# A gated cross-attention block: one slot's scores and the rounding of w1 are moved in the start-up, and the rounding takes two operations

## The chip, the core and the metric

The kernel runs on one core of a Trainium2 chip. The core has five engines with an in-order queue of instructions each: TensorE (PE, matrix products and transposes), VectorE (DVE), ScalarE (ACT), GpSimd (POOL) and SyncE (SP, which here only starts transfers). They meet by semaphores. The metric is the time of one execution on the device in microseconds (us).

## The reference

A Flamingo block: 16 batches of 224 tokens of width 512 attend to 750 context rows of width 384 each, of which a mask keeps a part (8 heads of 64); then comes a feed-forward net whose two weights are rounded to -1, 0 and 1 and whose activations are rounded to 8 bits.

```python
def weight_quant(w):
    scale = 1.0 / jnp.clip(jnp.mean(jnp.abs(w)), 1e-05)
    return jnp.clip(jnp.round(w * scale), -1.0, 1.0) / scale
def bitlinear(x, w, b):                       # act_quant: 127 steps to each row's largest
    return jnp.einsum('bsd,fd->bsf', act_quant(rmsnorm(x)), weight_quant(w)) + b
x = x + tanh(g_xattn) * xattn(layernorm(x), ctx, mask, W_q, W_k, W_v, W_o, b_o)
y = layernorm(x)                              # w1: 2048 x 512, w2: 512 x 2048
x = x + tanh(g_ffn) * bitlinear(gelu(bitlinear(y, w1, b1)), w2, b2)
```

## The kernel before, in words

**Slots.** A first stage (`order_batches`, with an SBUF pool `sel` of its own) sorts the 16 batches by how many context rows they keep, into 16 slots: eight of up to 192 kept rows, eight of up to 128. From then on only kept rows are loaded: `select` (indicators L816, key numbers L833, mask L845; its small products L822 on PE) works out a slot's rows, `gather` (L856) fetches them with indirect DMAs that POOL issues, and `fetch` does so for tokens (L793).

**A slot.** Tokens are handled in pairs of 128-row tiles that run across slots. `norm` layer-normalises a pair (statistics on the DVE, L952 and L953; the rest on POOL: L956, L959, a power L780 and the normalisation L961); `norm_first` does slot 0's on its own. `turn` (L987) transposes a tile on PE, `query_pieces` makes the queries (L1008), `context_pieces` transposes context rows (L881) and makes keys (L892) and values (L907, and L918 for rows above 128). `scores(s, n)` takes unit n of four, 112 tokens by four heads: products `sim` on PE (L1047), scaled, masked and with its maximum taken in one DVE instruction per head (L1061), the exponential with its sum on ACT (L1071), the sums' reciprocals on the DVE (L1080), and the product of both on POOL (L1081), all in a buffer `p`. `turn_probs` transposes a `p` on PE (L1101, L1108), `weighted` multiplies by the values. Pairs of 128 rows then go through projection (L1189), a second norm, `up` (L1259), the gelu, and `down` (L1304).

**Weights.** w1 and w2 come in eight chunks of 128 x 1024 float32 each. A chunk of w2 takes over the buffer `raw` of a w1 chunk once that is rounded. `sum_weights` adds up absolute values (even chunks on the DVE, L1363, odd ones on ACT, L1367, whose elementwise output goes to a scratch tile `junk`); `scale_weights` adds the sums over partitions with a product on PE (`wtotp`, L1375) and makes the scale `sw`. `round_weights` (L1396 to L1398) rounds a chunk into `w16`, of which there are three; `turn_weights` transposes it on PE (L1409 for w1, L1413 for w2) into the 8-bit weights `w1T`, `w2T` (copies L766 on ACT or L763 on the DVE: `evict` takes the one with the smaller running sum, `load["s"]` and `load["v"]`).

**The order.** The start is written out: fetch, select and gather of slot 0, its norm, loads of w1, queries, keys and values; slot 0's scores 0 and 1; the sums of w1 and its scale; then slot 1's norm pieces and `select(2)`; then the remaining loads (wo, bo, b1, b2). After that a loop runs over slots. In a slot s, `merge` interleaves three lists of pieces by their costs: `attention_pieces(s)` (with scores 2 and 3 of the slot between the turns), the preparation of the following slots, and, for s of 0 and 1, `weight_pieces(s)` (w1 with slot 0, w2 with slot 1), from slot 2 on the projection and the feed-forward net. At its end come scores 0 and 1 of slot s + 1. At s = 2 bo and b2 are multiplied by the gates on POOL (L1519, L1520).

This order of calls isn't yet the engines' order. The framework's scheduler places each engine's instructions in its queue by their readiness in its own model, so an instruction written later may come earlier, and `tc.issue_after(i)` holds those written under it behind instruction i. In the built kernel before, POOL's queue after p of units 0 and 1 holds: statistics and normalisation of x_1, two gathers of slot 2, the multiply of bo, that of b2, the normalisation of x_2, four indirect loads, then p of units 2 and 3.

Of the kernel before, what the change touches and what calls it, by code (L numbers as in the profile page):

```python
# [8 lines left out]
F32 = mybir.dt.float32  # L9
BF16 = mybir.dt.bfloat16  # L10
AF = mybir.ActivationFunctionType
ALU = mybir.AluOpType
# [17 lines left out]
def order_batches(ctx, tc, sh, mask, x, context):  # L30

    nc = tc.nc
# [3 lines left out]
    NJ = 6  # L36
    TJ = J // NJ
    const = sh.const
    sel = ctx.enter_context(tc.tile_pool(name="sel", bufs=1))
    ps = ctx.enter_context(tc.tile_pool(name="ps_sel", bufs=1, space=bass.MemoryType.PSUM))  # L40

    m8 = sel.tile([B, J], mask.dtype, name="m8")
# [683 lines left out]
def compact_path(ctx, tc, sh, x, context, out, late_loads):  # L726

    nc = tc.nc
    P = 128
    B, S, D = x.shape  # L730
    _, J, C = context.shape
    FF = sh.FF
    NQ = 2
    TQ = S // NQ
# [9 lines left out]
    I32 = mybir.dt.int32  # L744
    I16 = mybir.dt.int16
# [3 lines left out]
    pa = ctx.enter_context(tc.tile_pool(name="pa", bufs=1))  # L749
# [3 lines left out]
    load = {"v": 0.0, "s": 0.0}  # L753

    latest = {}
# [15 lines left out]
    def wide(shape, dtype, name):  # L771
        return ps_sim.tile(shape, dtype, tag="sim", name=name)
# [9 lines left out]
    def small(name, n=2):  # L782
        return pa.tile([P, n], F32, tag=f"s{n}", name=name, bufs=24 if n == 2 else 6)
# [181 lines left out]
    def norm_first(k):  # L965

        xp = normed[0]
        st = small(f"bs_x0_{k}", 6)
        nc.vector.bn_stats(st, xp[:, k, :])
        mv = small(f"mv_x0_{k}", 4)  # L970
        nc.vector.bn_aggr(mv[:, :2], st)
        rstd = small(f"rs_x0_{k}")
        nc.vector.tensor_scalar(rstd[:, :1], mv[:, 1:2], EPS, None, ALU.add)
        power = nc.gpsimd.tensor_tensor(rstd[:, :1], rstd[:, :1], sh.mhalf[:, :1], ALU.pow)
        nc.vector.tensor_scalar(xp[:, k, :], xp[:, k, :], mv[:, 0:1], rstd[:, :1], ALU.subtract, ALU.mult)
        return power.ins

    def slot_xnT(s):
        if "xnT" not in live[s]:
# [57 lines left out]
    def scores(s, n):  # L1037
        st = live[s]
        cap = CAPS[s]
        q, u = UNITS[n]  # L1040
        sim = wide([TQ, 2, 2, 256], F32, f"sim_{s}_{n}")

        begin = P if cap > P else 0
        for i in range(2):
            p = 2 * u + i
            for j in range(2):
                nc.tensor.matmul(  # L1047
                    sim[:, j, i, :cap],
                    lhsT=st["qT"][j * DH : (j + 1) * DH, p, q * TQ : (q + 1) * TQ],
                    rhs=st["kT"][j * DH : (j + 1) * DH, p, j * begin : j * begin + cap],  # L1050
                    start=True,
                    stop=True,
                )
        probs = pa.tile([TQ, 4, 192], F32, tag="p", name=f"p_{s}_{n}", bufs=3)
        total = small(f"sum_{s}_{n}", 4)
        for i in range(2):
            for j in range(2):
                h = 2 * i + j
                nmax = pa.tile([TQ, 1], F32, tag="nm", name=f"nm_{s}_{n}_{h}", bufs=12)

                nc.vector.tensor_tensor_reduce(  # L1061
                    out=probs[:, h, :cap],
                    in0=sim[:, j, i, :cap],
                    in1=st["mask"][:, j * begin : j * begin + cap],
                    scale=-(DH**-0.5),
                    scalar=FMAX,
                    op0=ALU.add,
                    op1=ALU.min,
                    accum_out=nmax,
                )  # L1070
                nc.scalar.activation(  # L1071
                    probs[:, h, :cap],
                    probs[:, h, :cap],
                    AF.Exp,
                    bias=nmax,
                    scale=-1.0,
                    accum_out=total[:TQ, h : h + 1],
                )
        rec = small(f"rec_{s}_{n}", 4)
        nc.vector.reciprocal(rec[:TQ], total[:TQ])  # L1080
        nc.gpsimd.tensor_tensor(  # L1081
            probs[:, :, :cap],
            probs[:, :, :cap],
            rec[:TQ].unsqueeze(2).to_broadcast([TQ, 4, cap]),
            ALU.mult,
        )
        load["v"] += 4 * (150 + 1.05 * cap + 83) + 150
        load["s"] += 4 * (250 + 0.96 * cap + 187)
        st["p", n] = probs

    def turn_probs(s, n):
        st = live[s]
        q, u = UNITS[n]
        cols = slice(q * TQ, (q + 1) * TQ)
        probs = st.pop(("p", n))
        if n == 0:
            st["pT"] = pa.tile([P, 12, S], F32, tag="pT", name=f"pT_{s}", bufs=1)
        pt = gen([P, 4, TQ], F32, f"ptp_{s}_{n}")
        for h in range(4):
            c = CAPS[s] - P if h % 2 else 0  # L1100
            nc.tensor.transpose(pt[:, h, :], probs[:, h, c : c + P], ident[:TQ, :TQ])  # L1101
        evict(st["pT"][:, 4 * u : 4 * u + 4, cols], pt, 4 * TQ)
        if CAPS[s] > P:

            pt = gen([P, 2, TQ], F32, f"ptr_{s}_{n}")
            for i in range(2):
                c = 2 * i * 192 + P
                nc.tensor.transpose(  # L1108
                    pt[:, i, :], probs.rearrange("t h k -> t (h k)")[:, c : c + P], ident[:TQ, :TQ]
                )  # L1110
            evict(st["pT"][:, 8 + 2 * u : 10 + 2 * u, cols], pt, 2 * TQ)
# [40 lines left out]
    def attention_pieces(s):  # L1152
        a = 4.0 if CAPS[s] > P else 2.6
        t = 0.8 if CAPS[s] > P else 0.5
        c = 1.4 if CAPS[s] > P else 1.0

        def both(n):
            scores(s, n)
            scores(s, n + 1)

        def wait():
            pass

        pieces = [(3.0, wait)]
        pieces += [(t, lambda n=n: turn_probs(s, n)) for n in (0, 1)]
        pieces += [(c, lambda: both(2)), (3.0, wait)]
        pieces += [(t, lambda n=n: turn_probs(s, n)) for n in (2, 3)]
        pieces += [(1.0, wait), (a, lambda: weighted(s))]
        return pieces
# [186 lines left out]
    def sum_weights(wi, c):  # L1356
        if c == 0:
            weight_sums.append(pa.tile([P, NPC], F32, name=f"wsums_{wi}"))
        if c == 1:
            late["junk"] = pa.tile([P, FF], F32, tag="h", name=f"junk_{wi}", bufs=2)  # L1360
        raw = raws[wi, c]
        if c % 2 == 0:
            nc.vector.tensor_reduce(  # L1363
                weight_sums[wi][:, c : c + 1], raw, AX.X, ALU.add, apply_absolute_value=True
            )
        else:
            nc.scalar.activation(late["junk"][:, :W], raw, AF.Abs, accum_out=weight_sums[wi][:, c : c + 1])  # L1367

    weight_scale = [None, None]
# [22 lines left out]
    def round_weights(wi, c):  # L1392

        raw = raws.pop((wi, c))
        quantised[wi, c] = w16 = pa.tile([P, W], BF16, tag="xq", name=f"w16_{wi}_{c}", bufs=3)
        nc.vector.tensor_scalar(raw, raw, weight_scale[wi], 1.0, ALU.mult, ALU.min)  # L1396
        nc.vector.tensor_scalar(w16.bitcast(I16), raw, -1.0, None, ALU.max)
        nc.vector.tensor_copy(w16, w16.bitcast(I16))  # L1398
        load["v"] += 1700

    def turn_weights(wi, c):
        w16 = quantised.pop((wi, c))
# [14 lines left out]
    def weight_pieces(wi):  # L1417

        p = []
        if wi == 1:  # L1420
            p += [(0.0, lambda: scale_weights(1))]
        for c in range(NPC + 2):
            if c < NPC:
                p += [(0.2, lambda c=c: round_weights(wi, c))]
                if wi == 0:
                    p += [(0.0, lambda c=c: load_weights(1, c))]
            if c > 1:
                p += [(0.6, lambda c=c: turn_weights(wi, c - 2))]
                if wi == 0:
                    p += [(0.0, lambda c=c: sum_weights(1, c - 2))]  # L1430
        return p
# [32 lines left out]
    select(0)  # L1464
    gather(0)
    select(1)
    norm_first(0)
    with tc.issue_after(norm_first(1)):
        fetch(1)
        gather(1)  # L1470
        fetch(2)
# [11 lines left out]
    with ExitStack() as behind:  # L1483
        for instruction in latest.values():
            behind.enter_context(tc.issue_after(instruction))
        scores(0, 0)
        scores(0, 1)
        for _, piece in queries[3:] + keys_values[3:]:
            piece()
        for c in range(NPC):  # L1490
            sum_weights(0, c)
        scale_weights(0)
        for _, piece in norm_pieces(1):
            piece()
        select(2)

        held = [sh.wo[0:1, 0, 0:1], sh.wo[0:1, 2, 0:1], sh.wo[P // 2 : P // 2 + 1, 2, 0:1]]
        for dst in held + [sh.bo[0:1, 0:1], sh.b1[0:1, 0:1], sh.b2[0:1, 0:1]]:
            nc.scalar.copy(dst, weight_sums[0][0:1, NPC - 1 : NPC])
# [85 lines left out]
```

## Time and profile before

| | |
|---|---|
| median of three runs | 756.2 us (754.46, 756.2, 758.74) |
| the profiled execution | 755.32 us |
| span of its trace | 753.5 us |
| mean granted PE clock | 0.976 of full speed |
| busy PE / DVE / ACT / POOL | 680.1 / 505.9 / 407.6 / 397.0 us |
| w1's last chunk landed, sums done | 36.0 us, 37.2 us |
| the queries (L1008) ahead of PE's longest wait | 54.28 to 57.38 us |
| PE's longest waits between 36 and 110 us | 5.1 for POOL's p, 3.6 for w2's first chunk, 1.7 for w1's first chunk |

Times are microseconds from the start of the span, unless marked ns. A line of a timeline gives start, length, engine, source line, operation, what is written and read with its shape, and how many instructions the line gathers. A line of waits gives who waits for whom: total, count and mean. A line of windows gives the stretch and its length, then the busy time of PE, of PE's weight loads, of DVE, ACT and POOL (instructions in brackets), the granted PE clock as a share of full speed, the share of the DMA engines and GB/s. The chain follows the work that ended last back from the end, each step to what released it; "issue" is time in which an engine waited for nothing that the profile shows. Numbers of buffers are left out of names (`x`, `raw`, `p`).

### The profile page before, as it was taken

The numbers are of one execution on the slowest core, as the hardware profiler recorded it, in microseconds if no ns is written. First come the engines' busy times: TensorE is split into PE (matmuls) and PEld (weight loads), VectorE is DVE, ScalarE is ACT, GpSimd is POOL, SyncE is SP. The second block draws the span as 40 slices with busy tenths as digits, with TensorE's granted clock in tenths as the row PEclk, the third lists the DMA queues.
The fourth block names the chain that finished last, engine by engine and source line by source line (L and its number), as shares of the span: only waits on it lengthen the run. The fifth ranks groups of instructions, "written<-read, shape, count | busy, mean of one in ns | idle before, by whom it ended". The sixth has DMA issues, their size and how long they took to land.

```text
span 753.5 us, 11378 instructions
## 1 busy us (share of the span) xinstructions
PE 680.1 (90%) x3902; PEld 432.9 (57%) x3902; DVE 505.9 (67%) x1300; ACT 407.6 (54%) x960; POOL 397.0 (53%) x543
## 2 busy tenths in 40 slices
PE   4997799999999999997999999999999999988652
PEld 3875587666566566555655575666666666443221
DVE  5598765877484784665768676588594939586860
ACT  1556564384663855736657369266565656460530
POOL 6583567464564644647266564565654453536141
PEclk9998999999999999999999999999999999999887
DMA  6874031132223322222142323123122222213150
GB/s 193 314 267 156 11 90 45 15 73 56 69 47 70 82 56 57 67 57 81 28 99 67 71 67 68 32 77 80 58 57 70 56 70 57 71 28 77 35 113 31
DMA packets 87218, 58.77 MB, mean 78 GB/s; under 512 B 75488, under 2 KB 75632, under 8 KB 87024
## 3 DMA queue, kind: packets, MB, share of 16 engines
q1 hardware_dynamic: 79024, 32.00, 18.8%
q0 software_dynamic: 8128, 25.96, 11.1%
q8 instruction: 33, 0.54, 0.3%
q14 instruction: 33, 0.27, 0.1%
HBM read 32.26 MB, written 7.34 MB: 53 GB/s over the span
## 4 chain that ended last, share of the span: by engine, by line
PE 57%; DVE 12%; issue 10%; POOL 9%; DMA 5%; ACT 2%; POOLq 0%; ACTq 0%; DVEq 0%; SPq 0%
PE qp L1008 9%; PE op L1189 9%; PE fp L1304 8%; PE hp L1259 6%; PE kp L892 5%; PE sim L1047 4%; PE vp L907 4%; PE ptp L1101 3%; PE av L1126 3%; DVE a L1282 2%; POOL p L1081 2%; DVE h L1267 2%; DMA raw<-in_L_ffn_w_dram 2%; DMA hqT<-hq 2%; DVE hq L1285 1%
## 5 line engine op out<-in xcount | busy, mean ns | idle before, releaser
L1081 POOL TENSOR_TENSOR p<-p,rec 112x768 f32<-112x768 f32 (+1 forms) x64 | 84.2, 1318 | 74.8 <-DVE rec L1080 29.6
L1304 PE MATMUL fp<-w2T,hqT 128*128 128x512 fp8e4 x448 | 104.2, 387 | 13.8 <-DMA hqT<-hq 13.7
L1259 PE MATMUL hp<-w1T,xqT 128*128 128x512 fp8e4 x448 | 107.0, 383 | 8.8 <-DVE h L1267 6.2
L1071 ACT ACTIVATE p<-p,nm 112x192 f32<-112x192 f32 (+1 forms) x256 | 106.4, 419 | 11.5 <-DVE nm L1061 11.3
L1008 PE MATMUL qp<-xnT,wq_sb 128*128 128x224 f32 x512 | 104.9, 358 | 0.6 <-ACT xnT L766 0.6
L1189 PE MATMUL op<-wo_sb,xoT 128*128 128x512 f32 x224 | 103.7, 599 | 0.0
L1008 PEld LDWEIGHTS qp<-xnT,wq_sb 128*128 128x128 f32 x512 | 96.8, 193 | 6.4 <-issue 3.3
L1267 DVE SCALAR_TENSOR_TENSOR h<-hp,c,b_bc 128x1024 f32<-128x1024 f32 x56 | 71.6, 1280 | 39.9 <-PE hp L1259 37.4
L1061 DVE CUSTOM_DVE_ANT_0 p<-sim,mask 112x192 f32<-112x192 f32 (+1 forms) x256 | 67.7, 319 | 33.9 <-PE sim L1047 33.4
L1304 PEld LDWEIGHTS <-hqT 128*128 128x128 bf16 x448 | 43.3, 99 | 71.0 <-DMA hqT<-hq 16.9
L1282 DVE TENSOR_REDUCE a<-h 128x1 f32<-128x2048 f32 x28 | 63.9, 2282 | 22.4 <-ACT h L1279 22.3
L1259 PEld LDWEIGHTS <-xqT 128*128 128x128 bf16 x448 | 43.2, 98 | 57.7 <-issue 15.4
L1308 DVE SCALAR_TENSOR_TENSOR y<-fp,c,y 128x512 f32<-128x512 f32 x28 | 20.9, 746 | 76.3 <-PE fp L1304 73.0
L1310 POOL DMA_INDIRECT out_dram<-y,token x28 | 30.9, 1104 | 75.6 <-DVE y L1308 70.6
L1290 ACT ACTIVATE h<-h 128x2048 f32<-128x2048 f32 x28 | 53.4, 1907 | 22.1 <-DVE hq L1285 14.7
L1279 ACT ACTIVATE h<-h 128x2048 f32<-128x2048 f32 x28 | 53.5, 1909 | 19.6 <-DVE k L1200 10.6
L1189 PEld LDWEIGHTS op<-wo_sb,xoT 128*128 128x128 f32 x224 | 40.6, 190 | 38.9 <-issue 36.4
L892 PE MATMUL kp<-ctxT,wk_sb 128*128 128x192 f32 (+1 forms) x384 | 60.9, 306 | 0.0
L892 PEld LDWEIGHTS kp<-ctxT,wk_sb 128*128 128x128 f32 x384 | 55.2, 192 | 6.2 <-issue 4.3
L1247 POOL TENSOR_TENSOR y<-y,b_bc 128x512 f32<-128x512 f32 x28 | 36.6, 1311 | 37.9 <-DVE fx L1228 37.6
L766 ACT COPY pT<-ptp 128x448 f32<-128x448 f32 x63 | 32.7, 536 | 42.6 <-PE ptp L1101 41.3
L1101 PE MATMUL ptp<-ident,p 112*128 112x112 f32 x256 | 36.1, 268 | 17.6 <-POOL p L1081 17.5
(165 smaller groups left out, 1191.4 us busy)
## 6 DMA issues: line engine op xcount, KB each, us to landing
raw<-in_L_ffn_w_dram SPq DMA_DIRECT2D x16, 512.0 KB, 5.6
wq_sb<-in_L_xattn_W_q_dram SPq DMA_DIRECT2D x1, 1024.0 KB, 5.8
b_bc<-in_L_ffn_b_dram SPq DMA_DIRECT2D x1, 1024.0 KB, 7.8
wk_sb<-in_L_xattn_W_k_dram SPq DMA_DIRECT2D x1, 768.0 KB, 7.4
wv_sb<-in_L_xattn_W_v_dram SPq DMA_DIRECT2D x1, 768.0 KB, 8.8
wo_sb<-in_L_xattn_W_o_dram SPq DMA_DIRECT2D x1, 512.0 KB, 3.8
wo_sb<-in_L_xattn_W_o_dram SPq DMA_DIRECT2D x2, 256.0 KB, 5.6
x<-in_x_dram,token POOLq DMA_INDIRECT x28, 3.6
```

What stands on the lines that cost most here:

```text
L892: nc.tensor.matmul(pk[:, p - p0, :], lhsT=sh.wk[:, c, p * P : (p + 1) * P], rhs=st["ctxT"][:, c, :cap], start=(c == 0), stop=(c == NC - 1),)
L1008: nc.tensor.matmul(pq[:, i, :], lhsT=sh.wq[:, d, (p + i) * P : (p + i + 1) * P], rhs=st["xnT"][:, d, :], start=(d == 0), stop=(d == ND - 1),)
L1061: nc.vector.tensor_tensor_reduce(out=probs[:, h, :cap], in0=sim[:, j, i, :cap], in1=st["mask"][:, j * begin : j * begin + cap], scale=-(DH ...
L1071: nc.scalar.activation(probs[:, h, :cap], probs[:, h, :cap], AF.Exp, bias=nmax, scale=-1.0, accum_out=total[:TQ, h : h + 1],)
L1081: nc.gpsimd.tensor_tensor(probs[:, :, :cap], probs[:, :, :cap], rec[:TQ].unsqueeze(2).to_broadcast([TQ, 4, cap]), ALU.mult,)
L1101: nc.tensor.transpose(pt[:, h, :], probs[:, h, c : c + P], ident[:TQ, :TQ])
L1189: nc.tensor.matmul(po, lhsT=xoT[:, d, at : at + P], rhs=sh.wo[:, d, :], start=(d == 0), stop=(d == ND - 1))
L1259: nc.tensor.matmul(ph[:, n, :], lhsT=f["xqT"][:, k * ND + d, :], rhs=w1T[:, d, at : at + NB], start=(d == 0), stop=(d == ND - 1),)
L1267: nc.vector.scalar_tensor_tensor(h[:, cols], ph.rearrange("t i n -> t (i n)"), f["c1", k], sh.b1[:, cols], ALU.mult, ALU.add)
L1279: nc.scalar.activation(f["h", k], f["h", k], AF.Gelu)
L1282: nc.vector.tensor_reduce(amax[:, k : k + 1], h, AX.X, ALU.max, apply_absolute_value=True)
L1304: nc.tensor.matmul(po, lhsT=f["hqT", k][:, n, :], rhs=w2T[:, n, :], start=(n == 0), stop=(n == NF - 1))
```

## The change

1. The pool `sel` of the sorting stage is taken from the other end of SBUF, so that its buffers lie apart from the first tokens' and context's.
2. `norm_first` also returns its last instruction: the second half of slot 0's tokens is normalised behind the first, and the fetches that follow are held behind the power in the second half.
3. `p` has four buffers in place of three.
4. Units 2 and 3 of slot 0's scores are called right behind its queries, keys and values, before the sums of w1; `attention_pieces(0)` has an empty piece in their place. The last DVE maximum of them is kept as `scored`.
5. Of w2's sums, chunks 0 and 4 are the DVE's and six are ACT's (before, four and four). w1's stay four and four.
6. Rounding: w times the scale into int32 (in the buffer `raw` itself), then the minimum with 1 and maximum with -1 into the bfloat16 `w16`. Before, there were three operations: scale and minimum in float32, maximum into int16, int16 to bfloat16. The planner's cost is 1400 instead of 1700.
7. The rounding of w1 is held behind `scored`.

```diff
--- before.py
+++ after.py
@@ -36,7 +36,8 @@
     NJ = 6
     TJ = J // NJ
     const = sh.const
-    sel = ctx.enter_context(tc.tile_pool(name="sel", bufs=1))
+
+    sel = ctx.enter_context(tc.tile_pool(name="sel", bufs=1, side="right"))
     ps = ctx.enter_context(tc.tile_pool(name="ps_sel", bufs=1, space=bass.MemoryType.PSUM))
 
     m8 = sel.tile([B, J], mask.dtype, name="m8")
@@ -972,8 +973,8 @@
         rstd = small(f"rs_x0_{k}")
         nc.vector.tensor_scalar(rstd[:, :1], mv[:, 1:2], EPS, None, ALU.add)
         power = nc.gpsimd.tensor_tensor(rstd[:, :1], rstd[:, :1], sh.mhalf[:, :1], ALU.pow)
-        nc.vector.tensor_scalar(xp[:, k, :], xp[:, k, :], mv[:, 0:1], rstd[:, :1], ALU.subtract, ALU.mult)
-        return power.ins
+        last = nc.vector.tensor_scalar(xp[:, k, :], xp[:, k, :], mv[:, 0:1], rstd[:, :1], ALU.subtract, ALU.mult)
+        return power.ins, last.ins
 
     def slot_xnT(s):
         if "xnT" not in live[s]:
@@ -1051,14 +1052,14 @@
                     start=True,
                     stop=True,
                 )
-        probs = pa.tile([TQ, 4, 192], F32, tag="p", name=f"p_{s}_{n}", bufs=3)
+        probs = pa.tile([TQ, 4, 192], F32, tag="p", name=f"p_{s}_{n}", bufs=4)
         total = small(f"sum_{s}_{n}", 4)
         for i in range(2):
             for j in range(2):
                 h = 2 * i + j
                 nmax = pa.tile([TQ, 1], F32, tag="nm", name=f"nm_{s}_{n}_{h}", bufs=12)
 
-                nc.vector.tensor_tensor_reduce(
+                latest["max"] = nc.vector.tensor_tensor_reduce(
                     out=probs[:, h, :cap],
                     in0=sim[:, j, i, :cap],
                     in1=st["mask"][:, j * begin : j * begin + cap],
@@ -1067,7 +1068,7 @@
                     op0=ALU.add,
                     op1=ALU.min,
                     accum_out=nmax,
-                )
+                ).ins
                 nc.scalar.activation(
                     probs[:, h, :cap],
                     probs[:, h, :cap],
@@ -1163,7 +1164,7 @@
 
         pieces = [(3.0, wait)]
         pieces += [(t, lambda n=n: turn_probs(s, n)) for n in (0, 1)]
-        pieces += [(c, lambda: both(2)), (3.0, wait)]
+        pieces += [(c, lambda: both(2) if s else wait()), (3.0, wait)]
         pieces += [(t, lambda n=n: turn_probs(s, n)) for n in (2, 3)]
         pieces += [(1.0, wait), (a, lambda: weighted(s))]
         return pieces
@@ -1359,7 +1360,7 @@
         if c == 1:
             late["junk"] = pa.tile([P, FF], F32, tag="h", name=f"junk_{wi}", bufs=2)
         raw = raws[wi, c]
-        if c % 2 == 0:
+        if c % (2 + 2 * wi) == 0:
             nc.vector.tensor_reduce(
                 weight_sums[wi][:, c : c + 1], raw, AX.X, ALU.add, apply_absolute_value=True
             )
@@ -1393,10 +1394,17 @@
 
         raw = raws.pop((wi, c))
         quantised[wi, c] = w16 = pa.tile([P, W], BF16, tag="xq", name=f"w16_{wi}_{c}", bufs=3)
-        nc.vector.tensor_scalar(raw, raw, weight_scale[wi], 1.0, ALU.mult, ALU.min)
-        nc.vector.tensor_scalar(w16.bitcast(I16), raw, -1.0, None, ALU.max)
-        nc.vector.tensor_copy(w16, w16.bitcast(I16))
-        load["v"] += 1700
+        nc.vector.tensor_scalar(raw.bitcast(I32), raw, weight_scale[wi], None, ALU.mult)
+        nc.vector.tensor_scalar(w16, raw.bitcast(I32), 1.0, -1.0, ALU.min, ALU.max)
+        load["v"] += 1400
+
+    def round_behind(wi, c):
+        if wi:
+            round_weights(wi, c)
+        else:
+
+            with tc.issue_after(scored):
+                round_weights(wi, c)
 
     def turn_weights(wi, c):
         w16 = quantised.pop((wi, c))
@@ -1421,7 +1429,7 @@
             p += [(0.0, lambda: scale_weights(1))]
         for c in range(NPC + 2):
             if c < NPC:
-                p += [(0.2, lambda c=c: round_weights(wi, c))]
+                p += [(0.2, lambda c=c: round_behind(wi, c))]
                 if wi == 0:
                     p += [(0.0, lambda c=c: load_weights(1, c))]
             if c > 1:
@@ -1464,8 +1472,10 @@
     select(0)
     gather(0)
     select(1)
-    norm_first(0)
-    with tc.issue_after(norm_first(1)):
+    _, normed_first = norm_first(0)
+    with tc.issue_after(normed_first):
+        power, _ = norm_first(1)
+    with tc.issue_after(power):
         fetch(1)
         gather(1)
         fetch(2)
@@ -1487,6 +1497,9 @@
         scores(0, 1)
         for _, piece in queries[3:] + keys_values[3:]:
             piece()
+        scores(0, 2)
+        scores(0, 3)
+        scored = latest["max"]
         for c in range(NPC):
             sum_weights(0, c)
         scale_weights(0)
```

## The prediction

> **What bounds the kernel now.** I read the busy times first, then the chain that ended last, then the waits of TensorE (PE) in the part that the diff touches, then the timelines of VectorE (DVE) and GpSimd (POOL) there, then windows for the clock.
>
> ```profile
> PE 680.1 (90%) x3902; PEld 432.9 (57%) x3902; DVE 505.9 (67%) x1300; ACT 407.6 (54%) x960; POOL 397.0 (53%) x543
> PE 57%; DVE 12%; issue 10%; POOL 9%; DMA 5%; ACT 2%; POOLq 0%; ACTq 0%; DVEq 0%; SPq 0%
> ```
>
> PE is the bound: from 110 to 690 us its slices are full. A change to the start is worth only the PE idle and slow-clock time that it adds or removes there; every later stage shifts by that sum. The chain in the start (start, length, engine, name):
>
> ```profile
> 20.36 15.63 DMA raw<-in_L_ffn_w_dram
> 36.07 1.16 ACT junk L1367 x2
> ...
> 57.66 1.02 POOL x L793
> 60.34 1.00 POOL ctx L856
> 61.36 1.49 POOL p L1081
> 62.90 1.01 PE ptp L1101 x4
> ```
>
> w1 lands at 36, its sums end at 37.2; later POOL's queue (fetches, then p of slot 0's heads 2 and 3) holds PE. PE's waits between 36 and 110 us (total, count, mean):
>
> ```profile
> PE ptp L1101 <- POOL p L1081: 5.1, 1, 5.1
> PE wp L1413 <- DVE w L1398: 3.6, 1, 3.6
> PE wp L1409 <- DVE w L1398: 1.7, 1, 1.7
> ```
>
> The clock around the first (span; PE, PE loads, DVE, ACT, POOL busy; PE clock; DMA; GB/s):
>
> ```profile
> 60.00:63.00 3.00, 0.10 (x1) 0.11 (x2) 3.00 (x3) 2.03 (x4) 2.67 (x4) 0.80 0.82 214
> 63.00:65.00 2.00, 2.00 (x10) 1.33 (x12) 2.00 (x2) 0.53 (x1) 1.26 (x1) 0.50 0.93 340
> ```
>
> PE ends its queries at 57.38, starts again at 62.90 (5.5 lost) and runs at 0.50 until about 68.6, so some 2.85 more is lost. After the 3.6 wait it runs at 0.50 from about 89.2 to 92.5, another 1.7.
>
> POOL and DVE there:
>
> ```profile
> 45.43 1.51 POOL L959 TENSOR_SCALAR ls_x<-mv_x 128x2 f32<-128x2 f32 x1
> 46.93 4.52 POOL L1519 TENSOR_SCALAR bo_bc<-bo_bc,tgates 128x512 f32<-128x512 f32 x1
> 52.18 1.55 POOL L1520 TENSOR_SCALAR b_bc<-b_bc,tgates 128x512 f32<-128x512 f32 x1
> ```
> ```profile
> 43.19 0.73 DVE L1396 TENSOR_SCALAR raw<-raw,sw 128x1024 f32<-128x1024 f32 x1
> 44.61 0.68 DVE L1397 TENSOR_SCALAR w<-raw 128x1024 int16<-128x1024 f32 x1
> 45.88 0.41 DVE L1398 CAST w<-w 128x1024 bf16<-128x1024 int16 x1
> 60.45 4.10 DVE L1398 CAST w<-w 128x1024 bf16<-128x1024 int16 x2
> ```
>
> The multiply L1519 takes 4.52 while rounding runs back to back (until 50.0); its twin L1520 takes 1.55. In reverse, two casts of 0.41 take 4.10 beside POOL's p.
>
> [...] The 0.50 windows after waits of 5.1 and 3.6 agree; after 1.7 it didn't fall. [...] No run here shows an int32 stream.
>
> **The change part by part.** Times are on the axis of before.
>
> *Two-step rounding.* Before, 0.73 + 0.68 + 0.41 = 1.82 a chunk; after, two passes. Bounds for one int32 pass: 0.41 (the cast's row) and 1.21 (the DVE sum of a chunk[...]); I take 0.67. A chunk then costs 1.34. w16 has three buffers, so the DVE can issue seven passes (raw 0 to 3, w 0 to 2) before w_3 waits for PE to have turned chunk 0.
>
> *Scores 2 and 3 of slot 0 moved.* Their 16 matmuls (2.1 us) move from PE's idle start-up to straight behind v_rest's; hidden there, since PE waits anyway for rounded weights. On the DVE eight maxes follow (0.28 each, 2.3). Before, the DVE starts raw_0 at 43.19. By the built order of the new kernel, ahead of raw_0 stand now: the maxes (41.5 to 43.8), a mask of slot 1, the six `ind` of slot 2 (0.25 each), four aggregates and keys. The maxes also feed POOL: its order becomes p_0, p_1, bo multiply (bo lands at 42.1), b2 multiply, p_2, two gathers, p_3, then rs, ls, pow of x_1 and x_2, x_1's two normalisations. Before, x_1 was normalised at 40.38, ahead of all that. Working: bo 42.1 to 43.6, b2 to 45.1 (the DVE's mask stands behind it), p_2 45.4 to 46.9 (the `ind` stand), so aggregates at 48.6 and raw_0 at 48.9, 5.7 later than before. POOL's gathers run 47.1 to 49.6; p_3 comes up at 49.65 and finds the DVE in 7 × 0.67 = 4.7 of back-to-back rounding: [...]it stands until 53.6, ends at 55.1; rs, ls and pow for both slots cost 2 × (0.29 + 0.19 + 0.72) = 2.4, the first normalisation 0.76: x_1's half 0 is ready at 58.4.
>
> *What that makes late.* The built order puts PE's four turns of x_1's half 0 (L987) ahead of the first turn of a rounded chunk (L1409). Before, they ran at 43.53. Now PE stands there: 58.4 − 43.5 = +14.9. The rounding lies fully behind that wait.
>
> *What it removes.* The 1.7 wait for the first chunk and the small gaps about it (−2.1): three chunks lie ready. The wait at 57.4 (5.5) and its slow clock (2.85): p_2 and p_3 are long done, −8.35. In return, the new idle of over 10 us puts PE at 0.50 on its first work: +2.3 (estimate: less than 2.85, since copies on ACT pace that part).
>
> *w2's stage.* Before, slot 1's last score ends at 83.68 and the first wp L1413 starts at 89.23. One pass of the first chunk goes: 5.55 becomes about 4.8 (−0.75), and the wait of about 2.9 would no longer reach the length after which the clock fell (−1.7). Two more of w2's sums go to ACT (1.25 each, 4 instead of 2 off the DVE's 1.21); ACT is idle half of that time, so nothing on PE; its price is 2.5 if one of them stands ahead of an eviction.
>
> *Start.* `sel` on the other side frees x_0's fetch from slots used by the sorting stage, but in the trace everything it waits for is over before POOL's own issue at 9.50; normed_first shifts x_0's halves against each other by under 0.5. Together −0.2. The fourth p buffer removes no wait that binds after the start; from slot 2 on the order is practically the old one: 0.
>
> Sum: +14.9 − 2.1 + 2.3 − 8.35 − 0.75 − 1.7 − 0.2 = +4.1. Against the profiled execution, 755.3 (span 753.5 and 1.8 around it): 759.4. The median is 0.9 above that execution, so 760.3.
>
> **The rivals.** The three runs shown lie 0.57% apart; I take 0.5% (752.4 to 760.0) as what a measurement of this kernel can tell from no change.
>
> A, the forecast: [...]PE waits for x_1. Over its sizes (int32 at 0.41: 1.8 earlier; a slow clock of 3.5 instead of 2.3) 758 to 763.
>
> B, on the other side: the DVE's rounding doesn't shut POOL out[...]. p_3 runs 49.65 to 51.1, x_1 is normalised at 54.3: +10.8 in place of +14.9, sum 0.0, time 756.2. From there up it is slower, below it faster. For it: no int32 row exists. Against: the 4.52.
>
> C: A, and w2's stage doesn't gain: [...]the clock falls again (+1.7), and an ACT sum delays an eviction (+2.5): 764. For it: the stage had 3.6 before; against: ACT's idle share.
>
> D: [...]Bo's and b2's multiplies, mask and `ind` overlap without loss, x_1 is ready at 50.5 (aggregates 48.6 less about 1.3, then 2.4 and 0.76): 7.0 − 2.1 + 2.3 − 8.35 − 2.65 = −3.8, time 752.4, and a little lower if the clock holds.
>
> That the change doesn't do what it says is excluded by the built order, which shows every move.
>
> **How the numbers follow.** A 0.48, B 0.30, C 0.13, D 0.09. The time is A's, 760.3. The range reaches from between D and B, 753.5, to C's 765. A lies across the upper bound: 0.30 of its chance above 760.0, 0.18 below. Slower 0.30 + 0.13 = 0.43; same 0.18 + 0.27 of B = 0.45; faster D and 0.03 of B = 0.12.
>
> **What would show it.** PE's waits in 36 to 70: one of some 12 to 15 us for L987 on POOL's x L961, with the clock at 0.50 after it; none for L1081. POOL's p_3 stretched to some 5 us beside back-to-back DVE passes of 0.67. If int32 passes take 1.2, or p_3 takes 1.5, it is B. At w2 a PE wait of about 2.9 and no 0.50 window; if that is there, C. I'd be wrong outright if PE's idle at x_1 is under 7 us, or if a wait past slot 2 differs by more than 1 us.

## The result, and the profile after

The changed kernel takes 765.05 us (median of 6 runs, 762.51 to 768.01) against 757.47 before in the same session: ratio 1.0106, 95% interval 1.0074 to 1.0139, so 5.6 to 10.5 us slower. The forecast was 760.3 with a range to 765.0. Its direction and its place were right; the size, +4.1, was about half of what came.

Line numbers after are higher than before, by one up to the rounding (L962 is the normalisation L961), by eight at the turns (L1417 and L1421 are L1409 and L1413) and by more than that at the gate multiplies (L1532 is L1519). p_n stands for the product p of unit n of a slot, x_1 for the token pair that is normalised for slot 1. The busy times and the chain that ended last, from the page after:

```profile
PE 684.4 (89%) x3902; PEld 436.3 (57%) x3902; DVE 500.9 (65%) x1284; ACT 407.3 (53%) x962; POOL 393.6 (51%) x543
PE 46%; issue 14%; DVE 13%; POOL 12%; DMA 5%; ACT 4%; POOLq 0%; ACTq 0%; DVEq 0%; SPq 0%
```

The DVE's busy time fell by 5.0 us; PE's share of the chain fell from 57% to 46%, as POOL's and "issue" rose. The chain in the start (start, length, engine, name):

```profile
43.71 1.00 POOL bo_bc L1532
...
46.82 1.46 POOL p L1082
48.44 1.36 POOL ctx L857
50.10 0.99 POOL ctx L857
51.12 1.48 POOL p L1082
...
56.11 0.76 POOL x L962
56.92 1.12 PE xnp L988 x4
```

This is POOL's queue ahead of x_1 (b2's multiply, at 45.25, lies in the first gap); before, x_1 stood in front of it all (40.38). PE's waits between 36 and 110 us follow (total, count and the longest one: the last figure of such a line is not a mean, as the text above has it):

```profile
PE xnp L988 <- POOL x L962: 9.3, 1, 9.3
PE pi L823 <- DVE ind L817: 4.1, 1, 4.1
PE wtotp L1376 <- DVE wtot L1374: 2.7, 1, 2.7
PE wp L1421 <- DVE w L1398: 1.6, 1, 1.6
```

The 5.1 for p is gone, 9.3 for x_1 (and 4.1 for the `ind` behind the maxima) stand in its place, and the wait for w2's sum has grown from 1.1 to 2.7. Before, that wait was

```profile
PE wtotp L1375 <- DVE wtot L1373: 1.1, 1, 1.1
```

Windows over the two gaps after, and then w2's start before (stretch, length; PE, loads, DVE, ACT, POOL busy; PE clock; DMA; GB/s):

```profile
50.00:57.00 7.00, 0.08 (x1) 0.08 (x2) 4.42 (x5) 0.00 (x0) 6.53 (x10) 0.50 0.83 248
57.00:62.00 5.00, 5.00 (x24) 4.60 (x25) 2.53 (x3) 2.46 (x5) 4.13 (x5) 0.50 0.30 89
...
92.00:95.00 3.00, 1.28 (x6) 0.91 (x6) 2.73 (x17) 1.26 (x5) 2.82 (x4) 0.63 0.00 0
95.00:100.00 5.00, 4.60 (x23) 4.26 (x24) 5.00 (x9) 2.33 (x6) 4.72 (x4) 0.54 0.00 0
```
```profile
89.00:93.00 4.00, 3.77 (x20) 3.43 (x21) 4.00 (x8) 1.88 (x4) 2.95 (x3) 0.57 0.04 7
```

PE stands until 56.9 and then works at half speed; and at w2's start (92.8 to 99.6) the clock is down again, for twice as long as before (89.1 to 92.5).

From here on I compare kernels at the first output that POOL issues, since every edit acts ahead of it and single executions differ a lot behind it (the profiled execution after is 2.7 above its median, the one before 2.2 below its own):

```profile
184.04 1.14 POOL L1310 DMA_INDIRECT out_dram<-y,token  x1 [0.17 <-DVE k L1200]
```
```profile
190.78 1.13 POOL L1311 DMA_INDIRECT out_dram<-y,token  x1 [0.17 <-DVE k L1201]
```

So +6.7 us, inside the interval of the runs: nearly all of the loss is made before the first output. By their last output these two executions are 12.4 apart, but e4 below, which has the same order on POOL in the start, takes 5.3 us less than the changed kernel from its first output to its last. So I don't count the further 5.7 as the change's; what makes it is not shown.

### The profile page after: what moved, and what is told of

It reads as the page before. It is cut to its first block, busy times and chain, and to the rows that moved or that the text cites. A ratio compares the mean times of both kernels' runs of the same rounds, so it can differ in the third digit from the quotient of the medians.

```text
span 766.0 us, 11366 instructions
## 1 busy us (share of the span) xinstructions
PE 684.4 (89%) x3902; PEld 436.3 (57%) x3902; DVE 500.9 (65%) x1284; ACT 407.3 (53%) x962; POOL 393.6 (51%) x543
## 4 chain that ended last, share of the span: by engine, by line
PE 46%; issue 14%; DVE 13%; POOL 12%; DMA 5%; ACT 4%; POOLq 0%; ACTq 0%; DVEq 0%; SPq 0%
PE op L1190 8%; PE qp L1009 8%; PE fp L1305 6%; PE hp L1260 6%; PE kp L893 4%; PE sim L1048 3%; PE vp L908 3%; DVE a L1283 3%; POOL p L1082 2%; DVE h L1268 2%; PE ptp L1102 2%; DMA raw<-in_L_ffn_w_dram 2%; PE av L1127 2%; DMA hqT<-hq 2%; DVE hq L1286 2%
## 5 line engine op out<-in xcount | busy, mean ns | idle before, releaser
L1305 PE MATMUL fp<-w2T,hqT 128*128 128x512 fp8e4 x448 | 107.6, 396 | 15.6 <-DMA hqT<-hq 15.6
L1260 PEld LDWEIGHTS <-xqT 128*128 128x128 bf16 x448 | 43.4, 98 | 57.0 <-issue 14.9
L893 PE MATMUL kp<-ctxT,wk_sb 128*128 128x192 f32 (+1 forms) x384 | 63.4, 314 | 0.0
L893 PEld LDWEIGHTS kp<-ctxT,wk_sb 128*128 128x128 f32 x384 | 57.9, 199 | 6.4 <-issue 4.5
L1048 PE MATMUL sim<-kT,qT 64*112 64x192 f32 (+1 forms) x512 | 50.2, 314 | 0.5 <-DVE h L1268 0.3
```

The lines of the kernel that those rows point to most:

```text
L893: nc.tensor.matmul(pk[:, p - p0, :], lhsT=sh.wk[:, c, p * P : (p + 1) * P], rhs=st["ctxT"][:, c, :cap], start=(c == 0), stop=(c == NC - 1),)
L1048: nc.tensor.matmul(sim[:, j, i, :cap], lhsT=st["qT"][j * DH : (j + 1) * DH, p, q * TQ : (q + 1) * TQ], rhs=st["kT"][j * DH : (j + 1) * DH, ...
L1260: nc.tensor.matmul(ph[:, n, :], lhsT=f["xqT"][:, k * ND + d, :], rhs=w1T[:, d, at : at + NB], start=(d == 0), stop=(d == ND - 1),)
L1305: nc.tensor.matmul(po, lhsT=f["hqT", k][:, n, :], rhs=w2T[:, n, :], start=(n == 0), stop=(n == NF - 1))
```

## The experiments

Theory Q: POOL's queue. x_1's normalisation now stands behind bo, b2, p_2, gathers and p_3; PE waits for it, gets part of that back later, and meets w2 with a slow clock. Rivals: R, the other parts of the change cost it; H, the held rounding would make PE wait anyway. Each ratio below is to the kernel before, run in the same session, with its 95% interval. The kernel before had medians of 756.46 to 760.23 in these sessions, so medians of different ones don't compare.

| kernel | first output, us | median, us | ratio |
|---|---|---|---|
| before / changed | 184.04 / 190.78 | 757.47 / 765.05 | 1.0106 (1.0074 to 1.0139) |
| e1, scores not moved | 180.51 | 753.43 | 0.9960 (0.9942 to 0.9978) |
| e2, scores moved alone | 191.23 | 764.09 | 1.0097 (1.0060 to 1.0135) |
| e3, x_1's norm ahead | 182.14 | 755.54 | 0.9976 (0.9955 to 0.9997) |
| e4, multiplies behind maxima | 190.74 | 763.50 | 1.0107 (1.0067 to 1.0147) |
| e5, PE kept busy at w2 | 190.98 | 765.16 | 1.0108 (1.0074 to 1.0142) |
| e6, multiplies behind p | 193.60 | 767.23 | 1.0144 (1.0107 to 1.0181) |
| e7, three-step rounding | 192.40 | 764.83 | 1.0118 (1.0082 to 1.0155) |
| e8, e3 and w2's scale ahead | 181.86 | 754.90 | 0.9989 (0.9970 to 1.0007) |
| e9, as e5, scores in place | 190.47 | 767.50 | 1.0151 (1.0107 to 1.0194) |
| e10, two-step rounding alone | 182.55 | 752.52 | 0.9938 (0.9915 to 0.9961) |
| e11, w2's sums even | 190.15 | 762.19 | 1.0083 (1.0056 to 1.0110) |
| e12, e1, scale and p ahead | 179.93 | 754.77 | 0.9965 (0.9942 to 0.9987) |
| e13, e8 and p ahead | 184.33 | 756.23 | 0.9963 (0.9939 to 0.9987) |
| e14, e10 and p ahead | 179.10 | 752.52 | 0.9911 (0.9889 to 0.9934) |
| e15, e14 and scale ahead | 179.97 | 751.84 | 0.9888 (0.9849 to 0.9928) |

A single first output carries the chance of its own start-up. PE starts the last values of slot 0 (L918) at 37.20 us in the kernel before, and 1.85 later in e10, 1.0 in e14 and 1.2 in e15, which have the same instructions up to there; e13 is 1.96 later than before and 1.6 later than the changed kernel.

**e1, the changed kernel without the moved scores** (parts 4 and 7 undone)

```diff
-        scores(0, 2)
-        scores(0, 3)
-        scored = latest["max"]
-        pieces += [(c, lambda: both(2) if s else wait()), (3.0, wait)]
+        pieces += [(c, lambda: both(2)), (3.0, wait)]
-                p += [(0.2, lambda c=c: round_behind(wi, c))]
+                p += [(0.2, lambda c=c: round_weights(wi, c))]
```

> The changed kernel with parts 4 and 7 undone: scores 2 and 3 of slot 0 stay between the turns, and the rounding isn't held; the start, the fourth p buffer, the sums of w2 and the two-step rounding stay. Theory Q (the loss comes from POOL's queue: x_1's normalisation stands behind bo, b2, p_2, p_3, so PE starts x_1's turns 13 us later, gets 8.4 back, and meets w2 with a slow clock): x_1's turns are back at about 43.5 to 44.5, PE's wait for POOL's p of some 5 us is back, time 753 to 758. Rival R (the other parts cost it: start, sums of w2, int32 passes): 762 or more.

753.43, and the sign turns: 0.996. PE's waits between 36 and 110 us are all small; the 5 us wait for p that I expected back isn't there. On POOL p_2 is done at 60.5 in place of 62.8, and bo's multiply, 4.52 before, took 1.57; why it got through is not shown. The two longest waits of PE are:

```profile
PE wp L1421 <- DVE w L1398: 1.8, 1, 1.8
PE wtotp L1376 <- DVE wtot L1374: 1.3, 1, 1.3
```

R falls: without the moved scores the rest of the change, the fourth buffer of `p` included, is a gain.

**e2, the moved scores alone** (kernel before; lines shortened)

```diff
+        scores(0, 2)
+        scores(0, 3)
         for c in range(NPC):
             sum_weights(0, c)
-        pieces += [(c, lambda: both(2)), (3.0, wait)]
+        pieces += [(c, lambda: both(2) if s else wait()), (3.0, wait)]
-        probs = pa.tile(..., tag="p", bufs=3)
+        probs = pa.tile(..., tag="p", bufs=4)
```

> The kernel before with scores 2 and 3 moved and the fourth p buffer that this needs, nothing else; POOL's queue is then that of the changed kernel. Q: PE's wait of about 9 to 12 us for x_1's normalisation appears here too, time 763 to 768 (a little above the changed kernel, since three-step rounding stretches the DVE stage by 0.5 a chunk). R: 755 to 759.

764.09, and the same wait appears:

```profile
PE xnp L987 <- POOL x L961: 9.7, 1, 9.7
```

This one edit reproduces the loss. It doesn't hold the rounding (part 7), and the rounding starts behind the eight maxima all the same, at 47.35 (47.87 in the changed kernel), so part 7 isn't needed for the loss.

**e3, x_1's norm written ahead of the moved scores**

```diff
+        for _, piece in norm_pieces(1):
+            piece()
         scores(0, 2)
         scores(0, 3)
...
-        for _, piece in norm_pieces(1):
-            piece()
```

> The changed kernel with one piece written earlier: x_1's norm (and its fetch) ahead of scores 2 and 3 instead of behind the scale of w1. In POOL's queue x_1's normalisation now stands ahead of bo, b2, p_2 and p_3. Q: x_1's turns at 43 to 45, then PE waits for the first rounded chunk until about 48 (rounding starts at 46 to 47 behind the maxima), no wait for POOL's p later; some 9 to 10 us earlier than the changed kernel at slot 1's scores; time 748 to 755. Rival H (the held rounding is what PE would wait for anyway): PE then stands at the first w1 turn until 55 or later, time 761 or more.

The wait for x_1 is gone, PE's first turn of w1 comes at 49.4 (57.8 in the changed kernel), and 8.6 us at the first output are back. That shows Q and refutes H. 755.54 is 0.5 over the range that I had given: H may have a small part, since the rounding starts 3.5 later than before, and w2's start is as slow as in the changed kernel. Nor do the moved scores gain anything in this better order: e1, which leaves them in place, is at 0.9960 and e3 at 0.9976. POOL's and the DVE's rows at 48 us:

```profile
48.08 5.25 POOL L857 DMA_INDIRECT ctx<-in_ctx_dram,keys  x1 [0.17 <-issue]
```
```profile
48.67 0.67 DVE L1398 TENSOR_SCALAR w<-raw 128x1024 bf16<-128x1024 int32 x1
49.27 1.40 DVE L1397 TENSOR_SCALAR raw<-raw,sw 128x1024 int32<-128x1024 f32 x2
50.59 1.28 DVE L1398 TENSOR_SCALAR w<-raw 128x1024 bf16<-128x1024 int32 x2
51.80 1.40 DVE L1397 TENSOR_SCALAR raw<-raw,sw 128x1024 int32<-128x1024 f32 x2
```

Beside seven int32 passes back to back POOL stands, as case A of the forecast had it for p_3: a gather's issue of 1.0 to 1.4 takes 5.25 and ends when the DVE pauses (53.2).

**e4 and e6, bo's and b2's multiplies out of the way**

```diff
+                with tc.issue_after(latest["max"]):   # e4: the latest maximum; e6: the latest product p
+                    nc.gpsimd.tensor_scalar(sh.bo, ...)
+                    nc.gpsimd.tensor_scalar(sh.b2, ...)
```

> The changed kernel with the multiplies of bo and b2 held behind slot 1's or 2's maxima, so that 3.2 us of POOL work and their hold on the DVE leave the queue ahead of x_1. Q: x_1 normalised 2 to 4 us earlier (53 to 55), PE's wait shorter by as much, time 760 to 763. R and H: no change, 764 to 766.

> The changed kernel with the multiplies of bo and b2 held behind POOL's own latest product p, which does take them out of the queue ahead of x_1 (holding them behind the DVE's maxima left the built order as it was). Theory Q: p_2 starts at 44.3 in place of 46.8, x_1's first turn comes 2 to 3.5 us earlier than 56.9, and the first output by as much (187.5 to 189). If p_3's place behind the DVE's rounding or the gathers decide alone, x_1 moves by under 1 us.

e4's edit left POOL's order as it was, so it doesn't test what it was made for and is a second sample of the changed kernel: 1.0107, first output 190.74. e6 does move them: x_1's wait falls from 9.3 to 6.8, and PE is 2.5 us ahead of the changed kernel until its first projection at 124.8. Then the residual, which adds bo, is late, and PE waits between 110 and 160 us:

```profile
PE ptp L1102 <- DVE y L1193: 3.6, 1, 3.6
```

Ahead of x_1 the multiplies cost 2.5, within the 2 to 3.5 that I expected, but in their new place they cost 5.3: this wait, and the queries behind it, which take 4.98 in place of 3.21.

**e7, three-step rounding in the changed kernel; e10, two steps in the kernel before** (the diff is e7's without the planner's cost, which goes with it; e10's is the reverse)

```diff
-        nc.vector.tensor_scalar(raw.bitcast(I32), raw, weight_scale[wi], None, ALU.mult)
-        nc.vector.tensor_scalar(w16, raw.bitcast(I32), 1.0, -1.0, ALU.min, ALU.max)
+        nc.vector.tensor_scalar(raw, raw, weight_scale[wi], 1.0, ALU.mult, ALU.min)
+        nc.vector.tensor_scalar(w16.bitcast(I16), raw, -1.0, None, ALU.max)
+        nc.vector.tensor_copy(w16, w16.bitcast(I16))
```

> The changed kernel with the rounding in three operations as before. The rounding of w1 lies behind PE's wait for x_1, so there only POOL's p_3 and x_1 can move (three buffers allow eight passes of 0.41 to 0.73 ahead of the first turn in place of seven, up to 0.5 later); at w2's start one operation more stands ahead of the first turn (0.4 to 0.8 later). First output 0.5 to 1.3 later than 190.8, time 765 to 767. If two steps are worth more than that over the sixteen chunks: over 768.

> The kernel before with nothing but the two-step rounding. PE's and POOL's queues stay as they were. First turn of w1 about 0.5 earlier, but the 5.1 wait for POOL's p stays or shrinks by 1 to 2, w2's first turn 0.8 to 1.5 earlier: first output 181 to 183.5 in place of 184.0, ratio 0.996 to 1.000. If it gives all of what the kernel without the moved scores gained (3.5), the sums of w2 and the start gave nothing.

In the changed kernel two steps gain 1.6 at the first output (192.40 to 190.78), more than I expected there, and make it at w2, where PE's wait for the first chunk is 3.0 in e7 and 1.6 in the changed kernel; the runs don't separate the two (1.0118 and 1.0106). Alone they gain 0.6% by the runs (0.4 to 0.85), beyond what I gave them: PE's wait for p falls from 5.1 to 3.0, and the clock after it is slow for 3.4 us in place of 6.8. That is the change's good part; e1, which has all parts but the moved scores and the hold, shows no more (0.9960).

**e11, w2's sums four and four**

```diff
-        if c % (2 + 2 * wi) == 0:
+        if c % 2 == 0:
```

> The changed kernel with w2's sums four and four again. Forecast: no gain from six on ACT, none lost. First output 190 to 191; if the three sums in a row on ACT at 66 to 72 us hold up PE's next turn, 189.5 to 190.3.

762.19. Six sums on ACT cost 0.6 at the first output, over half of which was there before w2's sums began; by the runs 0.2%, with overlapping intervals. At most a small loss.

**e5 and e9, PE kept busy at w2's start.** Products of 128x512 that nobody reads fill PE's gaps there (lines shortened).

```diff
+            for _ in range(3):                  # ahead of the turn of w2's first chunk
+                nc.tensor.matmul(wp_as_f32, lhsT=sh.wo[:, 0, :P], rhs=sh.wo[:, 1, :], start=True, stop=True)
+            for _ in range(4):                  # e5: ahead of wtotp; e9: two, behind slot 1's last score
+                nc.tensor.matmul(extra, lhsT=sh.wo[:, 0, :P], rhs=sh.wo[:, 1, :], start=True, stop=True)
```

> The changed kernel with seven products of 128x512 that nobody reads, in PE's two gaps at w2's start: four between slot 1's last score and wtotp, three ahead of the turn of w2's first chunk. PE then works through both gaps, and nothing else changes. If the failed step is the clock (the two gaps together bring PE to half speed from 93.4 to 100.2 us, some 2.4 us of work), the clock stays full there and the first output leaves POOL 1.5 to 2.5 us earlier than in the changed kernel (190.8), the time 0.2 to 0.4% below it. If the clock there costs nothing, the first output is at 190.8 or, as the products delay real work, up to 0.5 later.

> The changed kernel with unread products of 128x512 on PE at w2's start, now without moving slot 1's scores: two behind its last score, three ahead of the turn of w2's first chunk. (In the first attempt the scheduler put scores 2 and 3 of slot 1 behind the extra products, 1.5 us of work that had lain in the gap.) POOL's p_2 and p_3 of slot 1 come out ahead of two fetches in this build, which favours PE. If the fallen clock at 93 to 100 us was what kept the time (forecast step w2: a credit of 1.7), the first output is at 188 to 188.8 in place of 190.8. If POOL's p or the rounding of w2 bounds the stage next, it is at 190 to 191.

The clock now stays full. In e9:

```profile
92.00:95.00 3.00, 3.00 (x12) 1.75 (x13) 2.87 (x19) 1.88 (x8) 2.76 (x4) 1.00 0.00 0
95.00:100.00 5.00, 5.00 (x30) 3.53 (x29) 5.00 (x9) 3.21 (x11) 4.89 (x4) 1.00 0.01 3
```

But the products start 1.8 late, behind a maximum, and w2's first turn comes 1.5 after the changed kernel's; by 103 us PE is 0.4 ahead. So the fallen clock is worth 1.9 in this stretch, read from one trace of each, and filling the gap costs most of it. In e5 PE was 2.4 ahead at 101 us and gave it all back by 110: scores 2 and 3 of slot 1, moved behind the products (1.5), and a wait for p (0.8). Neither gains by the runs (1.0108 and 1.0151).

**e8, w2's scale ahead of slot 1's scores** (on e3)

```diff
-        if wi == 1:
-            p += [(0.0, lambda: scale_weights(1))]     # at the start of w2's pieces
+        if wi == 0:
+            p += [(0.0, lambda: scale_weights(1))]     # at the end of w1's pieces
```

> The kernel of the experiment with x_1's norm ahead, and the scale of w2 written at the end of w1's pieces instead of the start of w2's, so that its sum over the DVE's partials no longer stands behind slot 1's sixteen maxima. If w2's start is bounded by that queue: PE's wait for wtotp (2.7) goes, the first turn of w2 comes 3 to 5 us earlier, the clock stays full, and the first output is at 176 to 179 in place of 182.1; time 748 to 752. If w2's sums themselves are late: no change, 182.

The first turn of w2 comes 6.7 earlier than in e3 with a full clock (its eight products take 0.61, 1.04 in the changed kernel), and by 112 us nothing is left. Two waits for POOL's p take it, and slow clock behind the first (3.4 us): 2.8, since the fetches and gathers of later slots are now issued ahead of p_1, and 1.2, where POOL itself waits for the DVE's reciprocal:

```profile
PE ptp L1102 <- POOL p L1082: 4.0, 2, 2.8
```

**e12 to e15, p ahead of the transfers on POOL** (the diff shows the gathers' part). e12 holds slot 1's fetches and gathers behind p_1; e13 and e15 hold the fetches behind p_1 and slot 3's gathers behind slot 1's p_3; e14 only the gathers. e12 and e13 have the scale ahead, on e1 and e3; e14 and e15 stand on the kernel before with the two-step rounding, e15 with the scale ahead.

```diff
-            other.append((0.0, lambda s=s: gather(s + 2)))      # at s = 1
+            with tc.issue_after(latest["pm"]):                  # behind slot 1's last product p
+                gather(3)
```

> A version from the experiments: the kernel with scores 2 and 3 left between the turns, the scale of w2 written ahead of slot 1's scores, and slot 1's fetches and gathers held behind its p_1 on POOL, so that p_1 doesn't stand behind 5 us of transfers' issue. w2's first turn 2 to 4 us earlier than in the kernel without the moved scores, no slow clock there, and p in time: first output 177 to 179.5 (that kernel: 180.5), ratio to before 0.990 to 0.996. If p or the rounding of w2 still binds at 100 to 112 us: 180 to 181.

> The kernel with x_1's norm and w2's scale ahead, and slot 1's fetches held behind p_1 on POOL, slot 3's gathers behind p_3. In the run with the scale ahead w2's first turn came 6.2 earlier and all of it was lost by 112 us to two waits for POOL's p (4.0). If POOL's queue (transfers ahead of p) takes it: those waits shrink by 2 to 4, first output at 177.5 to 180 in place of 181.9, ratio 0.990 to 0.997. If p waits for the DVE (its sums and reciprocals lie between passes of rounding): 181 to 182.5, no gain.

> The kernel before with the two-step rounding and slot 3's gathers moved behind slot 1's p_3 on POOL, nothing else. They then no longer stand ahead of slot 0's p_2 and slot 1's p_2. PE's wait for p at 59 to 63 us (3.0) shrinks by about 1.4 to 2.7 and the slow clock after it goes; first output 1.5 to 4 earlier than with the two steps alone (182.6, of which 1.8 is that execution's late start), ratio 0.989 to 0.994. If the gathers are needed before slot 3's keys: no gain or a loss.

> The same with w2's scale written ahead of slot 1's scores and slot 1's fetches behind p_1. If w2's start and POOL's queue are the two bounds left before 112 us: first output 176 to 179, ratio 0.985 to 0.992. If only one of them is: as the run with the gathers moved alone.

e14 takes 0.9911 and e15 0.9888, the lowest ratios; their intervals overlap each other's and e10's, so the runs show no sure gain over the two steps alone. In the traces, less the late start-ups, the first output is at 180.7 in e10, 178.1 in e14 and 178.8 in e15. In e15 the waits for p between 36 and 110 us have shrunk to 0.8:

```profile
PE ptp L1101 <- POOL p L1081: 0.8, 1, 0.8
```

e12 and e13 missed. In e12 four gathers stand ahead of p_2 and PE waits 3.3 for it. In e13 no transfer stands ahead of p_3, but POOL waits 2.4 for the DVE's reciprocal, which stands there behind int32 passes of the rounding, and PE waits 2.2:

```profile
98.61 1.50 POOL L1082 TENSOR_TENSOR p<-p,rec 112x768 f32<-112x768 f32 x1 [2.40 <-DVE rec L1081]
```

That is the second branch of its expectation. At PE's work of 112 us e13 is 3.2 ahead of the kernel before in spite of its late start-up, e8 2.1; by 125 us e13 has lost it to gaps of 1.3 for which the trace names no cause and to the next wait for p (1.9, slot 2's). So where w2 starts early, p is the next bound between 86 and 103 us (e8, e12, e13), now by POOL's transfers (e8's first wait, e12), now by the DVE's queue (e8's second, e13); e15 over e14 shows no sure gain from w2's start.

## Why the prediction missed

By the steps of its sum, with the offsets of PE's work in the trace after against before, taken at the points that the forecast named:

| step | forecast | measured |
|---|---|---|
| x_1's turns start later | +14.9 | +13.4 (43.53 to 56.92) |
| w1's wait gone, own slow clock, wait for p and its clock gone (to the end of slot 1's last score) | -8.15 | -7.3 (83.68 to 89.81) |
| w2's first turn behind slot 1's last score | -0.75 | 0.0 (5.55 and 5.59) |
| clock at w2 | -1.7 | +0.5 |
| start and rest to the first output | -0.2 | +0.1 |
| sum | +4.1 | +6.7 |

**The place was right.** The maxima ran at 41.9 to 44.2 (forecast 41.5 to 43.8), POOL's queue was the one named, PE stood where it was said to, and e2 and e3 show that this wait makes the loss: one adds it to the kernel before, the other takes it out of the changed one.

**Its inner cause was wrong by place.** I had p_3 stand beside the rounding until 53.6, as bo's multiply had stood before (4.52); for int32 passes no run had shown it. POOL got in after four passes, and it was the DVE that stood, 3.01 for two passes of 0.7:

```profile
51.12 1.48 POOL L1082 TENSOR_TENSOR p<-p,rec 112x768 f32<-112x768 f32 x1
```
```profile
50.81 3.01 DVE L1397 TENSOR_SCALAR raw<-raw,sw 128x1024 int32<-128x1024 f32 x2
```

In exchange bo's multiply came 1.6 later than I put it (43.69), and the four small operations for x_1 and x_2 took 0.19 to 0.58 in place of 0.19 and 0.29. That x_1 was late by nearly the right amount is partly luck: here the DVE stood (3.01) and POOL ran through (1.48), in e3 POOL stood (5.25). What decides which of the two stands is not shown.

**The step that failed is w2's stage**, forecast -2.45 and measured +0.5; the other steps' errors nearly cancel. Two terms were wrong.

(1) The credit of 1.7 for the clock. I gave it because I put the wait at 2.9; before, the clock had fallen at the end of a wait of 3.6 (89.1) and not at one of 1.7, and that it would stay up at 2.9 was an estimate. In these traces shorter waits had a fall. In the changed kernel the clock fell at 92.79, right behind the wait of 2.7 and ahead of the second (1.6); in e6 it fell 0.1 us before such a wait of 2.7 was over; in e10 0.5 us into the second of two waits of 1.1 and 2.1:

```profile
84.50:85.00 0.50, 0.00 (x0) 0.00 (x0) 0.50 (x5) 0.47 (x1) 0.42 (x3) 1.00 0.00 0
85.00:85.50 0.50, 0.00 (x0) 0.00 (x0) 0.50 (x3) 0.12 (x1) 0.50 (x1) 0.50 0.00 0
```

What sets the moment of a fall is not shown. In the changed kernel the clock stayed down for 6.8 us, and e9 prices that at 1.9.

(2) The length of the stage, left to the rounding alone. It was 4.8 in the forecast and 5.59 in the trace, no shorter than before (5.55): PE's wait for w2's first chunk fell from 3.6 to 1.6, but its wait for w2's sum rose from 1.1 to 2.7, and its turns of x between them ran at half speed (four in 1.07, in 0.63 before). Slot 1's unit 0, whose products PE did at 67 us before, now follows at 85 with unit 1's, so that fourteen of slot 1's sixteen maxima run on the DVE from 86.0 to 92.2, right ahead of w2's sum; before, four of the twelve ahead of it were done at 69 to 71. The built order had shown this, and I had not priced it. Every kernel that leaves the start of w2 alone agrees: with the moved scores this wait is 2.7 (e2, e3, e4, e6, e7, e11), without them 1.1 to 1.3 (before, e1, e10, e14).

Two figures of the forecast don't come out of its own lines either: it lets the wait for p cost 5.5, though PE still turned a chunk of w1 until 57.81 and the wait was 5.1, which is half of the second row's error; and C's terms sum to 764.5, not 764.

Rival C was the nearest: the clock fell again and the stage gained nothing, though PE's longest wait there was 2.7, and its sum on ACT (2.5) showed as 0.6 at most. B's course held for p_3, which ran through in 1.48, not for the time. What remains of the 765.05 after the first output (+0.9 to +1.3 by the medians and the ratio) lies inside the interval; the two kernels that share the moved scores' queue, e2 and e4, are at +6.8 and +7.1 at their last output.

**Not priced enough: the gain of two steps.** I took 0.75 at w2; alone they are worth 0.6% of the whole, and with the moved scores the whole change is a loss.

## What to carry to other kernels

When work is moved ahead, list what each in-order queue that it feeds now holds ahead of its old first item: here two moved scores put two products, two multiplies and two gathers on POOL in front of one normalisation of 0.76 us, and PE waited 9.3 for it. Writing that normalisation first got back 8.6 us at the first output. A gain at an early stage counts only up to the next queue: twice here 2.5 us (e6) and 6.7 us (e8) were there in the trace and gone at a later wait, by 133 and 102 us.

## What the runs showed of the hardware

- int32 passes on the DVE took as long as float32 ones: 128x1024 took 0.73 from float32 to int32 and 0.68 from int32 to bfloat16 in the changed kernel (0.73 and 0.68 for the float32 steps before). The forecast's 0.67 a pass was an estimate: no row of before showed an int32 pass.
- An indirect gather's issue on POOL stood beside the DVE too: it took 5.25 in place of 1.0 to 1.4, beside seven such passes (e3). In the changed kernel two gathers beside four such passes took 1.36 and 0.99.
- PE's clock fell to half right behind a single wait of 2.7 us (changed kernel), just before the end of one (e6), and 0.5 us into the second of two waits of 1.1 and 2.1 (e10). Behind 60 us, the slow spells that I read lasted 3.4 us (before at 89.1, e1, e8, e12, e14), 6.8 (before at 61.8, the changed kernel, e2, e3, e4, e6, e11) or 10.2 (e7). With idle products in the gaps the clock stayed full (e5, e9).
